# A transformer decoder layer on one core: first loads on ScalarE's queue, one batch's tokens fetched earlier, one weight load cut in four

## The chip, the core and the metric

The kernel runs on one NeuronCore of one Trainium2 chip. A core has TensorE (PE: matrix products into PSUM), VectorE (DVE), ScalarE (ACT), GpSimd (POOL) and SyncE (SP), which run side by side and wait for each other by semaphores. Loads and stores between HBM and SBUF are issued by SP or ACT into a queue each and carried out by the core's 16 DMA engines. The metric is the device time of one launch in microseconds (us): the median of runs without a profiler. Times inside an execution come from one profiled execution, counted from its span's start.

## The reference

One decoder layer in f32: x (16 batches of 512 tokens of 256), then three parts, each with a residual and a layer norm.

```
# self-attention without softmax, 16 heads of 16, K = 2
q  = x + x @ Wq + bq
ks = x + x @ Wk[k] + bk[k];  vs = x + x @ Wv[k] + bv[k]      (both / 32)
state = prod_k( ks[k]^T vs[k] )  per head;  out = layernorm(q @ state) * g + b;  out = out @ Wo + bo
x = layernorm(x + out)
# cross-attention, 16 heads of 64, 64 context rows per batch
q = x @ Wq.T;  k, v = split(context @ Wkv.T);  out = softmax(q k^T / 8) v;  out = out @ Wout.T + b_out
x = layernorm(x + out)
# 8 experts, each takes the first 1024 tokens with a positive routing weight
w = softmax(x @ router_w.T + router_b)
x = layernorm(x + sum_e w[:, e] * relu(x @ inter[e]) @ outw[e])
```

## The kernel before

Everything is f32. Nothing is looped on the chip in the main part: Python writes the whole layer out, batch by batch. A batch's 512 tokens are 4 tiles of 128. Weights and per-batch products are folded where they can be: the self-attention state is built from the Gram matrix of a batch's tokens (`gram`: `ps_g`, in two passes at L634 and L639, and a transpose `ps_gt`, L650), times Wk (`ps_gk`), times Wv (`ps_s`), masked to heads (`state`, L744 and L745), and folded with Wq into one matrix (`ps_m`, L757), which multiplies the transposed tokens (`ps_o`, L775). Keys of the cross-attention (`ps_kv`, L511, from the transposed context `cT` and transposed rows of Wkv, `wT`) are made for all batches in the first 110 us and stored to DRAM (`k_dram`); so are the values times Wout (`vo_dram`). The cross-attention reads them back per batch (`ps_sim`, `ps_x`). Experts (`ps_h` L1077, `ps_e` L1094) run on the first two batches' tokens, held in SBUF as `x2_head` and, transposed, `head_T`.

What sets the order of instructions: six generators ("streams": grams, context, self-attention, cross-attention, routing, experts) yield between pieces of work. `weave` always advances the stream whose due time (`plan`) is earliest, among those that a small cost model (`Model`) holds to be ready; `until(lambda: made(t))` makes a stream yield until the model thinks that tile t is there. The model has its own notion of when a load lands: a load issued by ACT is there 5 us later, one issued by SP early on adds up in a line. `in_order` then fixes the resulting order on PE, DVE, ACT and POOL. DMA issues on SP are not part of that; SP takes its own in the order that the tile framework gives, one after another, each waiting for what it needs, among them the DMA semaphore that it takes over from an earlier DMA (eight of them are handed round).

The steps that matter here, with lines of this version:

- L218 loads ACT's function table as ACT's first instruction.
- L359 loads batch b's tokens for its Gram matrix (`gx`); batch 0 in four pieces, at the very start. Batch 1's load is the sixth of SP.
- L1239 issues the first two context tiles (`cn`, L490) and the first two tiles of Wkv's rows (`nat`, L500), 512 KB each, alternately, all on SP behind batch 0's `gx`.
- `key_weights` (L386) and, as the streams run, `rest_of_weights` (L424) load the other weights.
- After batch 1's Gram matrix, `finish_key_weights` and `router_columns` prepare Wk and the router's columns.
- `self_attention` loads a batch's tokens again, `xt` (L694), right ahead of their use; batch 0 needs them for a transpose on PE (L249) and for the residual.
- `routing(0)` (L966) closes the pool `setup`, opens the pool `ffn` in its room and loads the first expert's inner weights `wi` (L1111, 1 MB) and outer weights `wo_` (L1116, 1 MB). The first of these two waits until all that used the old room is done.
- `experts` waits, in the model, for both weights, and then writes out eight blocks of 128 inner features, 2 matmuls each, per 256 tokens.

Of the kernel before, what the change touches and what calls it, by code (L numbers as in the profile page):

```python
# [18 lines left out]
P = 128  # L19
# [105 lines left out]
def decoder_layer(  # L125
# [25 lines left out]
    nc = tc.nc  # L151
# [12 lines left out]
    E, _, FF = w_inter.shape  # L164
    NF = FF // P
# [48 lines left out]
        return t  # L214

    nc.scalar.preload_act_table_set("natural_log_exp_and_others")  # L218
    ident = const.tile([P, P], FP, tag="ident", name="ident")
    make_identity(nc, ident)  # L220
    eps = const.tile([P, 1], FP, tag="eps", name="eps")
# [107 lines left out]
    with ExitStack() as att:  # L329
# [66 lines left out]
        def finish_key_weights():  # L396
            for k in range(K):
                plus_identity(wk[:, :, k, :])

            nc.vector.tensor_scalar_mul(nbk, nbk, float(S))  # L400
# [5 lines left out]
            out=hm, in_=hm, pattern=[[0, NC], [-HD, P // HD], [0, HD]], compare_op=ALU.is_ge,  # L406
# [3 lines left out]
            out=hm, in_=hm, pattern=[[0, NC], [HD, P // HD], [0, HD]], compare_op=ALU.is_ge,  # L410
# [74 lines left out]

        BJ = B * J

        def load_context(sp, q):
            t = wk2.tile([P, 4, C], FP, tag="vo", name="cn", bufs=6)
            nc.sync.dma_start(  # L490
                out=t,
                in_=context.rearrange("b j c -> (b j) c")[q * 512:(q + 1) * 512, :].rearrange(
                    "(i p) c -> p i c", p=P
                ),
            )
            return t

        def load_wkv(sp, r4):
            t = wk2.tile([P, 4, C], FP, tag="vo", name="nat", bufs=6)
            nc.sync.dma_start(out=t, in_=x_wkv[r4 * 512:(r4 + 1) * 512, :].rearrange("(r p) c -> p r c", p=P))  # L500
            return t

        NG = 512 // (GB * J)
# [183 lines left out]
                    sums[b // QB][1].append(key_sums(sums["u4"]))  # L687
                    yield WAIT

        grams, sums, x_blocks = {}, {}, {}  # L690

        def load_x(b):
            t = wk1.tile([P, NT, CX], FP, tag="xt", name="xt")
            nc.sync.dma_start(out=t[:, :, :C], in_=x[b].rearrange("(t p) c -> p t c", p=P))  # L694
            return t

        def self_attention(b, done):
# [47 lines left out]
            nc.vector.scalar_tensor_tensor(state, state, STATE_SCALE, headmask, ALU.mult, ALU.mult)  # L745

            yield from until(lambda: finished["x1"] >= b)
            xt = load_x(b)
            if b < FIRST:
                yield from until(lambda: made(xt))  # L750
                transposed(xT.rearrange("p t c n -> p c t n"), xt, lambda t: t)
# [212 lines left out]
        head_T, first_expert, ffn = {}, [], None  # L964

        def routing(b, x1):  # L966

            nonlocal ffn
            x2 = x2_head[:, b] if b < HEAD_B else x1
            yield from normalized(x2, lambda t: x1[:, t, :])  # L970
            yield WAIT
            if b == 0:

                yield from until(lambda: ("values", 1) in held)
                setup.close()
                ffn = pool(att, "ffn", 1)
                first_expert.extend((load_inter(0), load_outer(0)))
            if b < HEAD_B:
                head_T[b] = ffn.tile([P, NC, S], FP, tag=f"head_T{b}", name="head_T", bufs=1)
                transposed(head_T[b], x2)  # L980
            yield
            w = w_all[:, b * NT:(b + 1) * NT, :]
            m = small.tile([P, NT], FP, tag="rm", name="rm")
            mbc = m.unsqueeze(2).to_broadcast([P, NT, E])
            nc.vector.tensor_add(w, x2[:, :, C:], cs["rb"].unsqueeze(1).to_broadcast([P, NT, E]))
            nc.vector.tensor_reduce(m, w, AX.X, ALU.max)
            nc.vector.tensor_sub(w, w, mbc)
            nc.scalar.activation(w, w, AF.Exp)
            yield WAIT
            nc.vector.tensor_reduce(m, w, AX.X, ALU.add)  # L990
            nc.vector.reciprocal(m, m)
            nc.vector.tensor_mul(w, w, mbc)
            if b >= HEAD_B:


                r0 = (b - HEAD_B) * S
                nc.sync.dma_start(out=x2_rest[r0:r0 + S, :].rearrange("(t p) c -> p t c", p=P), in_=x2[:, :, :C])
                yield from normalized(x2[:, :, :C], lambda t: x2[:, t, :C])
                nc.sync.dma_start(out=out[b].rearrange("(t p) c -> p t c", p=P), in_=x2[:, :, :C])
            yield  # L1000
# [59 lines left out]
        def experts():  # L1060

            wi = wo_ = None
            yield from until(lambda: 0 in head_T and made(head_T[0]))
            for e in range(E):
                if e == 0:
                    wi, wo_ = first_expert
                    yield from until(lambda: made(wi, wo_))
                for n in range(CAP // TB):  # L1070
                    b, t0 = divmod(n * TB // P, NT)
                    yield from until(lambda: b in head_T and made(head_T[b]))
                    hT = []
                    for f in range(NF):
                        ps = bank("ps_h")
                        for cc in range(NC):
                            nc.tensor.matmul(  # L1077
                                ps[:, :TB], wi[:, cc, f * P:(f + 1) * P],
                                head_T[b][:, cc, t0 * P:t0 * P + TB], start=(cc == 0), stop=(cc == NC - 1),
                            )  # L1080
                        h = ffn.tile([P, TB], FP, tag="hT", name="hT", bufs=12)
                        if scalar_first():
                            nc.scalar.activation(h, ps[:, :TB], AF.Relu)  # L1083
                        else:
                            nc.vector.tensor_relu(h, ps[:, :TB])
                        hT.append(h)
                        yield
                    if n == CAP // TB - 1 and e + 1 < E:
                        wi = load_inter(e + 1)
                    yield from until(lambda: finished["routing"] > b)  # L1090
                    for t in range(TB // P):
                        ps = bank("ps_e")
                        for f in range(NF):
                            nc.tensor.matmul(  # L1094
                                ps[:, :C], hT[f][:, t * P:(t + 1) * P], wo_[:, f, :],
                                start=(f == 0), stop=(f == NF - 1),
                            )
                            if f % 4 == 3:
                                yield
                        acc = x2_head[:, b, t0 + t, :C]  # L1100
                        nc.vector.scalar_tensor_tensor(
                            acc, ps[:, :C], w_all[:, b * NT + t0 + t, e:e + 1], acc, ALU.mult, ALU.add
                        )
                        if e == E - 1:
                            beside(experts_st, last_norm(b, t0 + t))
                    if n == CAP // TB - 1 and e + 1 < E:
                        wo_ = load_outer(e + 1)

        def load_inter(e):
            t = ffn.tile([P, NC, FF], FP, tag="wi", name="wi", bufs=1)  # L1110
            nc.sync.dma_start(out=t, in_=w_inter[e].rearrange("(c p) f -> p c f", p=P))  # L1111
            return t

        def load_outer(e):
            t = ffn.tile([P, NF, C], FP, tag="wo_", name="wo_", bufs=1)
            nc.sync.dma_start(out=t, in_=w_out[e].rearrange("(f p) c -> p f c", p=P))  # L1116
            return t
# [60 lines left out]
        def made(*tiles):  # L1178
            return all(model.made[t.name][0] <= model.free["PE"] for t in tiles)

        def until(ready):
            while not ready():
                yield 0.5

        def all_grams():
            for b in range(B):
                if b >= QB:
                    grams_st.plan(SETUP + (b - QB - 0.8) * STEP, STEP, 2.9)
                yield from until(lambda: finished["states"] > b - 5)
                yield from grams_of([b])  # L1190
                if b == 1:
                    yield from until(lambda: made(early, wk, nbk))
                    finish_key_weights()
                    yield from router_columns(rw)
                    yield
                if b == QB - 1:
                    cs.update(rest_of_weights(sp))
                    yield
                    yield from until(lambda: made(early, wo, wv))
                    finish_weights()  # L1200
                    yield WAIT
                    yield from router_weights(sp)
# [33 lines left out]

        setup = ExitStack()
        sp = pool(setup, "setup", 2)
        nats = [load(sp, q) for q in range(2) for load in (load_context, load_wkv)]  # L1239
        gram_x[1] = load_gram_x(1)  # L1240
        key_weights()
        cs = {}
# [49 lines left out]
    with tc.For_i(0, n, 1) as i:  # L1292
# [6 lines left out]
        for e in range(E):  # L1299
            wi, wo_ = expert_weights(e)  # L1300
# [43 lines left out]
```

## Time and profile before

| | |
|---|---|
| three runs | 1355.06, 1355.67, 1358.25 us |
| median | 1355.67 us |
| the profiled execution | 1358.28 us, of which the span 1356.3 us |
| mean granted TensorE clock over the span | 0.996 |
| HBM read, written | 127.29 MB, 49.81 MB |
| DMA, mean over the span | 132 GB/s |

The page gives busy time by engine, the chain of work that ended last, followed back from the last instruction, the costliest groups of instructions, and DMA issues with the time from issue to landing. A row of the timeline reads: start in us, how long the group lasted, engine, source line, operation, what it writes and reads, count, and in brackets the idle time of its engine ahead of it and what ended that. PEld is the load of weights into PE, SPq and ACTq are the queues' issues. A window row gives the stretch, its length, busy time of PE, PEld, DVE, ACT and POOL (with the number of instructions), the granted TensorE clock, the DMA engines' busy share and GB/s. Some lines from the start, where the loads named above stand:

```profile
0.82 1.82 SPq L359 DMA_DIRECT2D gx<-in_x_dram  x4
...
3.16 0.51 SPq L500 DMA_DIRECT2D nat<-in_L_xattn_Wkv_dram  x1
3.71 0.51 SPq L490 DMA_DIRECT2D cn<-in_ctx_dram  x1
4.26 0.51 SPq L500 DMA_DIRECT2D nat<-in_L_xattn_Wkv_dram  x1
...
59.39 1.06 PE L249 MATMUL ps_t<-ident,xt 128*128 128x128 f32 x8 [1.35 <-DMA xt<-in_x_dram]
```

### The profile page before, as it was taken

To read this page: it belongs to the slowest core of one execution; us is meant where nothing else is said; L and a number is where in the kernel's file an instruction comes from. 1 tells how busy PE (TensorE), PEld (TensorE's weight loads), DVE (VectorE), ACT (ScalarE), POOL (GpSimd) and SP (SyncE) were. 2 spreads that over 40 slices of the span, in tenths; PEclk is the share of its full clock that TensorE was granted. 3 is DMA by queue.
4 is the path that set the end of the run, shared out by engine and by line. 5 is a ranking of instruction groups with operands and counts; after the bars stand their busy time and mean duration, and the time that the engine had idled before them with its cause. 6 is when DMAs were issued, how large, how long until landed. Compare 5 with 4: busy or idle time off the path is not lost.

```text
span 1356.3 us, 23928 instructions
## 1 busy us (share of the span) xinstructions
PE 1334.3 (98%) x9438; PEld 1052.6 (78%) x9438; DVE 817.4 (60%) x1961; ACT 422.5 (31%) x970; POOL 204.2 (15%) x140
## 2 busy tenths in 40 slices
PE   8999998999999999999999999999999999999997
PEld 5676675887788787887788787877788787878796
DVE  1265837556474747567555758566655848474844
ACT  2244424242222514143222414142323304142323
POOL 0010201112021111202021111202111112112100
PEclk9999998999999999999999999999999999999999
DMA  8737474421535353723645353623635153605411
GB/s 264 210 128 241 159 225 157 118 74 41 151 119 150 110 152 96 205 70 112 172 128 142 95 154 124 185 64 110 182 88 155 63 160 109 176 30 126 129 56 41
DMA packets 115204, 178.73 MB, mean 132 GB/s; under 512 B 17032, under 2 KB 83856, under 8 KB 115088
## 3 DMA queue, kind: packets, MB, share of 16 engines
q1 hardware_dynamic: 97808, 151.98, 39.1%
q10 hardware_dynamic: 17280, 25.17, 5.5%
q8 instruction: 76, 1.25, 0.4%
q14 instruction: 40, 0.33, 0.1%
HBM read 127.29 MB, written 49.81 MB: 131 GB/s over the span
## 4 chain that ended last, share of the span: by engine, by line
PE 93%; DVE 4%; DMA 1%; issue 1%; ACT 1%; SPq 0%; POOL 0%; POOLq 0%; DVEq 0%; ACTq 0%
PE ps_x L954 17%; PE ps_h L1077 16%; PE ps_sim L933 15%; PE ps_e L1094 15%; PE ps_p L799 4%; PE ps_o L775 4%; PE ps_kv L511 4%; PE ps_gk L712 4%; PE ps_vo L571 2%; PE ps_kq L862 2%; PE ps_s L724 2%; PE ps_g L634 2%; PE ps_m L757 1%; PE ps_zt L788 1%; PE ps_g L639 1%; PE ps_t L249 1%
## 5 line engine op out<-in xcount | busy, mean ns | idle before, releaser
L1077 PE MATMUL ps_h<-head_T,wi 128*128 128x256 f32 x1024 | 243.4, 383 | 4.0 <-issue 4.0
L933 PE MATMUL ps_sim<-kq,x1T 128*128 128x512 f32 x512 | 237.8, 593 | 0.0
L1077 PEld LDWEIGHTS ps_h<-head_T,wi 128*128 128x128 f32 x1024 | 194.2, 192 | 49.8 <-issue 20.9
L954 PE MATMUL ps_x<-vo,pT 32*128 32x264 f32 x4096 | 232.5, 383 | 0.2 <-DVE off L321 0.2
L954 PEld LDWEIGHTS ps_x<-vo,pT 32*128 32x128 f32 x4096 | 209.5, 185 | 20.8 <-issue 2.3
L920 POOL TENSOR_TENSOR s<-s,sm 128x1024 f32<-128x1024 f32 x64 | 121.7, 1901 | 650.2 <-DVE sm L919 572.5
L961 DVE TENSOR_TENSOR x<-ps_x,x 128x264 f32<-128x264 f32 x64 | 23.2, 425 | 234.9 <-PE ps_x L954 234.9
L1083 ACT ACTIVATE hT<-ps_h 128x256 f32<-128x256 f32 x177 | 67.7, 382 | 302.3 <-PE ps_h L1077 266.8
L933 PEld LDWEIGHTS ps_sim<-kq,x1T 128*128 128x128 f32 x512 | 96.2, 190 | 77.7 <-issue 69.8
L939 DVE TENSOR_REDUCE mx<-ps_sim 128x8 f32<-128x512 f32 x128 | 86.2, 674 | 59.4 <-PE ps_sim L933 58.6
L911 ACT ACTIVATE s<-s 128x512 f32<-128x512 f32 x128 | 79.3, 624 | 88.9 <-DVE s L940 68.9
L940 DVE TENSOR_TENSOR s<-ps_sim,mx 128x512 f32<-128x512 f32 x128 | 88.5, 692 | 4.4
L922 DVE STREAM_TRANSPOSE pT<-s 128x1024 f32<-128x1024 f32 x64 | 78.5, 1226 | 4.5 <-POOL s L920 4.2
L918 DVE TENSOR_REDUCE sm<-s 128x16 f32<-128x1024 f32 x64 | 76.5, 1196 | 0.0
L324 ACT ACTIVATE x<-x,off,rstd 128x264 f32<-128x264 f32 (+1 forms) x112 | 58.4, 592 | 33.9 <-DVE off L321 29.5
L775 PE MATMUL ps_o<-m,xT 128*128 128x264 f32 x256 | 63.6, 389 | 0.0
L799 PE MATMUL ps_p<-wo,zT 128*128 128x264 f32 x256 | 62.0, 387 | 0.0
L799 PEld LDWEIGHTS ps_p<-wo,zT 128*128 128x128 f32 x256 | 48.5, 190 | 15.4 <-issue 6.6
L511 PE MATMUL ps_kv<-cT,wT 128*128 128x512 f32 x128 | 59.6, 596 | 0.3
L835 POOL TENSOR_TENSOR x<-x,bout 128x1056 f32<-128x1056 f32 x16 | 39.1, 2446 | 136.4 <-PE ps_t L249 43.2
L712 PE MATMUL ps_gk<-wk,g 128*128 128x256 f32 x256 | 59.4, 379 | 0.0
L712 PEld LDWEIGHTS ps_gk<-wk,g 128*128 128x128 f32 x256 | 48.5, 190 | 11.2 <-issue 4.9
(178 smaller groups left out, 1739.8 us busy)
## 6 DMA issues: line engine op xcount, KB each, us to landing
vo<-vo_dram SPq DMA_DIRECT2D x512, 132.0 KB, 4.1
vo_dram<-vst SPq DMA_DIRECT2D x64, 264.0 KB, 2.8
x_blocks<-xb ACTq DMA_DIRECT2D x24, 512.0 KB, 3.3
xt<-in_x_dram SPq DMA_DIRECT2D x16, 512.0 KB, 3.8
wi<-L_ffn_experts_inter_dram SPq DMA_DIRECT2D x8, 1024.0 KB, 4.8
x_rest<-x SPq DMA_DIRECT2D x14, 512.0 KB, 3.1
out_dram<-x SPq DMA_DIRECT2D x14, 512.0 KB, 4.5
gx<-in_x_dram SPq DMA_DIRECT2D x52, 128.0 KB, 3.8
```

Of the source, the lines that this page charges most:

```text
L511: nc.tensor.matmul(ps, wT[:, cc, r % 4 * P:(r % 4 + 1) * P], cT[:, cc, q * 512:(q + 1) * 512], start=(cc == 0), stop=(cc == NC - 1),)
L712: nc.tensor.matmul(ps[:, :C], blk, wk[:, j, k, :], start=(j == 0), stop=(j == NC - 1))
L775: nc.tensor.matmul(ps[:, :CX], xT[:, t, cc], m[:, cc, :], start=(cc == 0), stop=(cc == NC - 1))
L799: nc.tensor.matmul(ps[:, :CX], zT[:, cc, t * P:(t + 1) * P], wo[:, cc, :], start=(cc == 0), stop=(cc == NC - 1))
L911: nc.scalar.activation(s[:, hs, :], s[:, hs, :], AF.Exp, scale=SCALE)
L920: nc.gpsimd.tensor_mul(s, s, sm.unsqueeze(2).to_broadcast([P, NH, J]))
L933: nc.tensor.matmul(ps, x1T[:, t, cc], kq[:, cc, hf * 512:(hf + 1) * 512], start=(cc == 0), stop=(cc == NC - 1),)
L939: nc.vector.tensor_reduce(mx[:, hs], sim, AX.X, ALU.max)
L940: nc.vector.tensor_sub(s[:, hs, :], sim, mx[:, hs].unsqueeze(2).to_broadcast([P, 8, J]))
L954: nc.tensor.matmul(ps[q][:, :CX], probsT[pq, blk].rearrange("p t i -> p (t i)"), vos[c][pq, i, :], start=(c == 0 and i == 0), stop=(c == 7 ...
L1077: nc.tensor.matmul(ps[:, :TB], wi[:, cc, f * P:(f + 1) * P], head_T[b][:, cc, t0 * P:t0 * P + TB], start=(cc == 0), stop=(cc == NC - 1),)
L1094: nc.tensor.matmul(ps[:, :C], hT[f][:, t * P:(t + 1) * P], wo_[:, f, :], start=(f == 0), stop=(f == NF - 1),)
```

## The change

Four edits. The first context tile and the first tile of Wkv's rows are issued by ACT instead of SP, as ACT's first instructions; ACT's table load follows them. Batch 0's tokens `xt` are loaded at the point where the router's columns are prepared, behind batch 1's Gram matrix, instead of inside `self_attention`. The first expert's `wi` is loaded in four pieces of 256 of its 1024 columns (the other experts' in one). `experts` no longer waits in the model for the first expert's weights.

```
-    nc.scalar.preload_act_table_set("natural_log_exp_and_others")
...
-        def load_context(sp, q):
+        def load_context(sp, q, eng=nc.sync):
             t = wk2.tile([P, 4, C], FP, tag="vo", name="cn", bufs=6)
-            nc.sync.dma_start(
+            eng.dma_start(
...
-        def load_wkv(sp, r4):
+        def load_wkv(sp, r4, eng=nc.sync):
             t = wk2.tile([P, 4, C], FP, tag="vo", name="nat", bufs=6)
-            nc.sync.dma_start(out=t, in_=x_wkv[r4 * 512:(r4 + 1) * 512, :].rearrange("(r p) c -> p r c", p=P))
+            eng.dma_start(out=t, in_=x_wkv[r4 * 512:(r4 + 1) * 512, :].rearrange("(r p) c -> p r c", p=P))
...
-        grams, sums, x_blocks = {}, {}, {}
+        grams, sums, x_blocks, first_x = {}, {}, {}, []
...
             yield from until(lambda: finished["x1"] >= b)
-            xt = load_x(b)
+            xt = first_x.pop() if b == 0 else load_x(b)
...
-                first_expert.extend((load_inter(0), load_outer(0)))
+                first_expert.extend((load_inter(0, NF // 2), load_outer(0)))
...
                 if e == 0:
                     wi, wo_ = first_expert
-                    yield from until(lambda: made(wi, wo_))
...
-        def load_inter(e):
+        def load_inter(e, pieces=1):
             t = ffn.tile([P, NC, FF], FP, tag="wi", name="wi", bufs=1)
-            nc.sync.dma_start(out=t, in_=w_inter[e].rearrange("(c p) f -> p c f", p=P))
+            n_ = FF // pieces
+            for i in range(pieces):
+                nc.sync.dma_start(
+                    out=t[:, :, i * n_:(i + 1) * n_],
+                    in_=w_inter[e, :, i * n_:(i + 1) * n_].rearrange("(c p) f -> p c f", p=P),
+                )
             return t
...
                     yield from until(lambda: made(early, wk, nbk))
+                    first_x.append(load_x(0))
                     finish_key_weights()
...
-        nats = [load(sp, q) for q in range(2) for load in (load_context, load_wkv)]
+        nats = [load(sp, q, (nc.scalar, nc.sync)[q]) for q in range(2) for load in (load_context, load_wkv)]
+
+        nc.scalar.preload_act_table_set("natural_log_exp_and_others")
```

## The prediction

> **What bounds the kernel now.** I read the page first (busy shares, chain that ended last), then TensorE's list of waits, then the timeline and stretches of windows around each wait.
>
> ```profile
> PE 1334.3 (98%) x9438; PEld 1052.6 (78%) x9438; DVE 817.4 (60%) x1961; ACT 422.5 (31%) x970; POOL 204.2 (15%) x140
> ...
> PE 93%; DVE 4%; DMA 1%; issue 1%; ACT 1%; SPq 0%; POOL 0%; POOLq 0%; DVEq 0%; ACTq 0%
> ```
>
> TensorE (PE) is busy for 98% of the span and makes 93% of the chain: 1356.3 - 1334.3 = 22 us of idle time is all that loads can give back, except where PE is busy but slow. Where it waits:
>
> ```profile
> PE ps_h L1077 <- issue: 4.0, 1, 4.0
> PE ps_g L634 <- DMA gx<-in_x_dram: 2.9, 1, 2.9
> PE ps_m L757 <- DVE state L745: 2.4, 2, 1.2
> PE ps_t L249 <- DMA cn<-in_ctx_dram: 1.8, 1, 1.8
> ...
> PE ps_t L249 <- DMA xt<-in_x_dram: 1.4, 1, 1.4
> ```
>
> The columns are total us, times, longest. Lines 1, 4 and 5 are the three waits that the three edits touch. The one called "issue" is the first expert:
>
> ```profile
> 214.62 0.38 SPq L1111 DMA_DIRECT2D wi<-L_ffn_experts_inter_dram  x1
> ...
> 216.13 0.68 DVE L201 COPY head_T<-ps_t 128x512 f32<-128x512 f32 x1
> ...
> 219.68 6.48 PE L1077 MATMUL ps_h<-head_T,wi 128*128 128x256 f32 x16 [4.05 <-issue]
> ```
>
> The load of wi is issued at 214.62 and takes 4.8 us (its row of the DMA issues); its landing at 219.42 is what releases PE, since the other operand is there at 216.81. PE has been idle since 215.63. Next, 16 matmuls take 6.48 us, which at the 379 ns and less of this line elsewhere (8 in 1.89 at 241.62) would be 3.6. The windows (last three columns: granted clock, DMA share, GB/s) say why:
>
> ```profile
> 218.00:218.50 0.50, 0.00 (x0) 0.00 (x0) 0.50 (x3) 0.00 (x0) 0.11 (x1) 0.99 1.01 418
> 218.50:219.00 0.50, 0.00 (x0) 0.00 (x0) 0.50 (x2) 0.00 (x0) 0.50 (x1) 0.50 1.01 406
> ...
> 225.00:225.50 0.50, 0.50 (x3) 0.42 (x2) 0.00 (x0) 0.33 (x2) 0.50 (x1) 0.68 0.37 123
> ```
>
> The granted clock falls to 0.50 at 218.49, 2.86 us after the last matmul, and is back at 225.32. From 219.68 to 225.32 PE works 5.64 us at half clock: 2.8 us lost over and above the wait. It is the only such place but the kernel's tail, where the clock falls 2.31 us after the last matmul (1349.41 to 1351.72).
>
> **The change, part by part.** Compared instruction by instruction, the built programs have the same order on DVE and POOL; PE has one group moved; ACT gains two DMA issues; SP's loads are re-ordered in the first 60 us, and wi becomes four. So with PE as the bound, what is taken from a PE wait moves the end by as much, if nothing is late in its place.
>
> *Batch 0's tokens (xt).* Before: issued at 54.71, landed 59.26, PE idle 1.35 us to 59.39. Now it is issued behind the third gx load, near 15 us, over 40 us early. Gain 1.35 us; bounds 0 and 1.35. What is late next is ps_m L757, which needs state (DVE, done at 59.68): PE would reach it at 58.04 + 2 x 0.9 = 59.8, so nothing. Its issue, 0.43 us, stands on SP ahead of the k_dram stores and two gx loads; their covers are long: the third gx landed near 20.4 (14.96 + 5.4) for use at 26.3, the fourth near 27 for 33.5, and k_dram is read back at 59.34 for PE at 124.4. The other SP moves (small rows, k_dram) have the same cover.
>
> *wi in four.* Piece 0 is 256 KB. No row shows such a load on an idle queue: the nearest are 128 KB (first gx piece, issued 0.82, used 2.92: 2.1 us) and 1024 KB (4.8 us). By the line between them a piece takes 2.1 + 2.7 / 7 = 2.5; I take 2.9, since in this load's own windows the first 250 KB had moved by 217.0, 2.4 us after issue. PE starts at about 217.75 instead of 219.68: 1.9 us. Bounds: 0 (it lands no sooner) and 2.8 (head_T at 216.81). Pieces 1 to 3 follow 0.4 us apart, against 1.7 us of matmuls a piece: covered. Three more issues put wo_ off from 215.05 to about 216.2; landed at 222.2, used first at 248.6. The dropped wait in experts() changes no order.
>
> *The half clock.* PE would be back 2.1 us after its last matmul. Known: the 1.83 us wait for cn left it fast (transposes after it 276 ns, 272 elsewhere); no fall came sooner than 2.31. I take no fall: 2.8 us saved; bounds 0 and 2.8.
>
> *First loads on ACT's queue.* Taken alone it removes the 1.83 us wait for cn and, as gram 1 now stands ahead of the four ps_kv, the 0.37 us wait for wT: best case 2.2 us. But see the start:
>
> ```profile
> 2.69 0.43 SPq L490 DMA_DIRECT2D cn<-in_ctx_dram  x1
> ...
> 4.81 1.28 SPq L359 DMA_DIRECT2D gx<-in_x_dram  x1
> ...
> 8.55 1.06 PE L249 MATMUL ps_t<-ident,cn 128*128 128x128 f32 x8 [1.83 <-DMA cn<-in_ctx_dram]
> ...
> 20.33 1.05 PE L639 MATMUL ps_g<-gx 128*128 128x129 f32 x8
> ```
>
> ```profile
> 2.00:3.00 1.00, 0.05 (x1) 0.08 (x1) 0.04 (x1) 0.10 (x1) 0.68 (x3) 1.00 0.79 247
> ...
> 4.00:5.00 1.00, 1.00 (x4) 0.82 (x3) 0.00 (x0) 0.00 (x0) 0.00 (x0) 1.00 0.51 142
> ...
> 6.00:7.00 1.00, 0.71 (x2) 0.00 (x0) 0.00 (x0) 0.00 (x0) 0.00 (x0) 1.00 1.05 372
> ```
>
> From 5 us on the DMA engines are full at some 372 GB/s; from 2 to 5 they moved 213 on average. A second queue fills that hole and no more: (372 - 213) x 3 us = 0.47 MB, or 1.2 us for everything behind. cn lands sooner, gram 0's pieces (now sharing with cn) a little later. nat, used at 10.34, must still come through 1.57 MB and half of the second cn: no gain. The second gx load is now wanted sooner: before, gram 1 ran at 15.15, after four ps_kv; now ahead of them, at 11.5. That load was issued at 4.81 and took 9.4 us: landed 14.2. Now its issue waits for cn's landing (the DMA semaphore it takes over), about 7 to 8 us, but behind fewer bytes: 14.2 - 1.2 = 13.0. Then gram 1 (1.74) and eight ps_kv (2 x 3.43) bring PE to L639 at 13.1 + 8.6 = 21.7, where it was at 20.4: 1.2 us worse. With the full best case, 2.2 better; with landing still at 14.2, 2.4 worse. I take a cost of 1.0. ACT's two issues (0.35 each by its x_blocks row) put its table load (1.28) off to end near 3; ACT's first copy is at 9.21: covered.
>
> The Trainium skill, "DMA: Bandwidth & Descriptors", section "Issuing engines are not separate DMA queues", says that loads issued from several engines run on the same 16 DMA engines and only save issue time. By that rule this edit would save no more than the 0.47 MB hole, as worked out from the windows; with queues of their own it would be the 2.2.
>
> *Sum.* -1.35 - 1.9 - 2.8 + 1.0 = -5.05 us. The profiled execution took 1358.28 (span 1356.3 and 2.0 around it): 1353.2. It lies 2.6 over the median of 1355.67 (runs 1355.06, 1355.67, 1358.25). I take that as a difference of the execution elsewhere and put the sum to the median, as a wait of 4.05 is longer than any after which the clock fell: 1355.67 - 5.05 = 1350.6.
>
> **The rivals.**
> A. The half clock isn't in the median. 2.6 is close to 2.8: the two quick runs may not have paid it, or the shorter wait still takes the clock down. Then 1355.67 - 1.35 - 1.9 + 1.0 = 1353.4. For it: one run of three lies at the profiled time. Against: those executions have the same 4.05 us wait. The three changes of clock lie 6.83 and 1126.40 us apart, 2 and 330 times 3.413: it is reviewed on a fixed beat. The Trainium skill, "TensorE: Matmul & The Clock Gate", Part 1, calls that beat free-running, not reset by a kernel; by that rule where the wait falls on it differs per execution, and A's time would come up in some of them.
> B. The start costs more: slower. The second gx lands as late as before, 14.2; PE has nothing from 11.48 on, 2.7 us; from 13.8 (11.48 + 2.31) the clock falls there too. 2.4 + 2.8 - 1.35 - 1.9, with the first expert still at half clock: +2.0, 1357.6. Against: the load stands behind fewer bytes.
> C. The start gives all its 2.2: 1355.67 - 1.35 - 1.9 - 2.8 - 2.2 = 1347.4. Needs the second gx by 10.5; 3.1 MB at 372 GB/s alone last till then.
> D. The pieces don't help: the first matmul still waits for all eight DMA semaphores in the program, and if piece 0 lands with the rest only xt counts: 1355.67 - 1.35 + 1.0 = 1355.3.
>
> **Chances.** Forecast 0.50 (its own range 1349 to 1352.3), A 0.27, B 0.06, C 0.10, D 0.07. The bound of 0.3% is 4.07 us (about what a measurement of this kernel tells from no change). Faster (below 1351.6): 0.45 of the forecast, C, 0.03 of A: 0.58. Slower: most of B, 0.05. The rest is 0.37. The range, 1347.4 to 1355.0, leaves out B, part of D and the end of C.
>
> **What would show it.** xt: no PE wait near 58. wi: ps_h starts about 2.1 us after PE's last transpose, granted clock 1.00 after it, 16 matmuls in 3.6 us. Start: cn's wait gone, a DMA wait of 1 to 2 us ahead of gram 1, L639 near 21.5. I am wrong if L639 comes before 19 or after 23, or if the clock falls all the same.

## The result, and the profile after

| | before | after |
|---|---|---|
| median | 1355.87 us (1355.06 to 1359.63, 13 runs) | 1353.3 us (1352.39 to 1354.16, 13 runs) |
| ratio, 95% interval | | 0.9975 (0.9967 to 0.9983) |
| profiled execution, its span | 1358.28, 1356.3 us | 1354.12, 1352.3 us |

The change takes 2.6 us off the median, less than the 4.07 us that were set as the bound of "no change". The interval of the ratio leaves out 1, so the kernel is faster, if by little. It was forecast to take 5.05.

The page of the changed kernel, busy time and engines of the chain that ended last:

```profile
PE 1333.8 (99%) x9438; PEld 1052.6 (78%) x9438; DVE 816.6 (60%) x1961; ACT 422.7 (31%) x970; POOL 204.3 (15%) x140
...
PE 94%; DVE 4%; ACT 1%; issue 0%; DMA 0%; POOL 0%; SPq 0%; POOLq 0%; DVEq 0%; ACTq 0%
```

TensorE's idle time went from 22.0 to 1352.3 - 1333.8 = 18.5 us, and its busy time fell by 0.5 only, though the first expert's half clock is gone: slow matmuls came up elsewhere. TensorE's list of waits of the changed kernel (total us, times, longest):

```profile
PE ps_g L632 <- DMA gx<-in_x_dram: 5.1, 3, 4.0
...
PE ps_h L1074 <- issue: 1.9, 1, 1.9
```

The rows for cn and xt are no longer there. The wait for wi fell from 4.0 to 1.9. Batch 0's tokens (gx) rose from one wait of 2.9 to three of 5.1. The first expert, from the timeline, and a window of it (last three columns: granted clock, DMA share, GB/s):

```profile
60.35 1.04 PE L247 MATMUL ps_t<-ident,xt 128*128 128x128 f32 x8
...
215.77 1.92 SPq L1110 DMA_DIRECT2D wi<-L_ffn_experts_inter_dram  x4
...
218.65 3.69 PE L1074 MATMUL ps_h<-head_T,wi 128*128 128x256 f32 x16 [1.89 <-issue]
```

```profile
217.50:218.50 1.00, 0.00 (x0) 0.00 (x0) 1.00 (x2) 0.00 (x0) 0.00 (x0) 1.00 1.03 363
```

The transposes of xt have no idle time ahead of them. ps_h comes 1.89 us after the last transpose instead of 4.05, the clock stays at 1.00, and the 16 matmuls take 3.69 us instead of 6.48. Now the start: TensorE's first matmuls before, then ACT's two issues and TensorE in the changed kernel:

```profile
2.95 3.77 PE L634 MATMUL ps_g<-gx 128*128 128x257 f32 x8 [2.95 <-DMA gx<-in_x_dram]
```

```profile
0.82 0.48 ACTq L488 DMA_DIRECT2D cn<-in_ctx_dram  x1
1.32 0.53 ACTq L498 DMA_DIRECT2D nat<-in_L_xattn_Wkv_dram  x1
...
3.96 1.20 PE L632 MATMUL ps_g<-gx 128*128 128x257 f32 x2 [3.96 <-DMA gx<-in_x_dram]
5.58 1.23 PE L632 MATMUL ps_g<-gx 128*128 128x257 f32 x2 [0.42 <-DMA gx<-in_x_dram]
7.50 2.08 PE L632 MATMUL ps_g<-gx 128*128 128x257 f32 x4 [0.70 <-DMA gx<-in_x_dram]
9.38 1.92 PE L247 MATMUL ps_t<-ident,cn 128*128 128x128 f32 x8
...
14.20 1.91 PE L632 MATMUL ps_g<-gx 128*128 128x257 f32 x8
...
22.80 1.05 PE L637 MATMUL ps_g<-gx 128*128 128x129 f32 x8
```

The DMA issues of the first 16 us, before and after (KB each, median us to landing), have batch 0's four pieces as:

```profile
gx<-in_x_dram SPq DMA_DIRECT2D x4, 128.0 KB, 2.3
```

```profile
gx<-in_x_dram SPq DMA_DIRECT2D x4, 128.0 KB, 4.3
```

Before, the first 8 matmuls started at 2.95 and ran without a gap. Now 1 MB is put on the DMA engines at 0.82 and 1.32 us, beside batch 0's four pieces of 128 KB: these come late, in three groups, and the matmuls after them still run at half speed (transposes 1.92 us for 8, 1.06 at full clock). The second pass of gram 1, L639 before and L637 now, is at 22.80 instead of 20.33: 2.5 us lost at the start. Gram 1 itself, at 14.20, waits for nothing; its load (issued 5.16, 6.9 us to landing) has been there since 12.03.

Of the difference of the profiled spans, 4.0 us, the start takes back what xt gives and more: x_head's transposes stand 1.1 us later than before. From there to the end of the first expert's first block the changed kernel wins 2.16 of wait and 2.8 of half clock.

### The profile page after: what moved, and what is told of

It reads as the page before. It is cut to its first block, busy times and chain, and to the rows that moved or that the text cites. A ratio compares the mean times of both kernels' runs of the same rounds, so it can differ in the third digit from the quotient of the medians.

```text
span 1352.3 us, 23937 instructions
## 1 busy us (share of the span) xinstructions
PE 1333.8 (99%) x9438; PEld 1052.6 (78%) x9438; DVE 816.6 (60%) x1961; ACT 422.7 (31%) x970; POOL 204.3 (15%) x140
## 3 DMA queue, kind: packets, MB, share of 16 engines
q8 instruction: 76, 1.25, 0.4%
## 4 chain that ended last, share of the span: by engine, by line
PE 94%; DVE 4%; ACT 1%; issue 0%; DMA 0%; POOL 0%; SPq 0%; POOLq 0%; DVEq 0%; ACTq 0%
PE ps_x L952 17%; PE ps_h L1074 16%; PE ps_sim L931 16%; PE ps_e L1091 15%; PE ps_p L797 4%; PE ps_kv L509 4%; PE ps_o L773 4%; PE ps_gk L710 4%; PE ps_vo L569 2%; PE ps_kq L860 2%; PE ps_s L722 2%; PE ps_g L632 2%; PE ps_m L755 1%; PE ps_g L637 1%; PE ps_zt L786 1%; PE ps_t L247 1%
## 5 line engine op out<-in xcount | busy, mean ns | idle before, releaser
L1074 PE MATMUL ps_h<-head_T,wi 128*128 128x256 f32 x1024 | 240.6, 380 | 1.9 <-issue 1.9
```

What stands on the lines that cost most here:

```text
L1074: nc.tensor.matmul(ps[:, :TB], wi[:, cc, f * P:(f + 1) * P], head_T[b][:, cc, t0 * P:t0 * P + TB], start=(cc == 0), stop=(cc == NC - 1),)
```

## The experiments

"Eight", "four" are the pieces of the first expert's wi; "start" is the edit with ACT's queue and the table load. Ratios are against runs of the kernel before on the same chip: runs 1 to 4 share one, 5 to 8 another, 9 to 11 a third, and 12 has a fourth.

**1. The kernel before, once more** (no edit).

> The kernel before, unchanged, to see how its executions differ. Theory: the half clock at the first expert (2.8 us) is paid in some executions and not, or less, in others, because the clock is reviewed on a fixed beat that a launch doesn't reset; then the runs spread over 1355.0 to 1359.6 us, the long ones (over 1357) have the lower mean granted clock (0.996) and the short ones a higher one (0.998 or more). Rival: the clock falls there in every execution and the spread is something else; then all runs show a mean clock near 0.996, whatever their time. Ratio 1.000 in both.

Measured: 1355.66 us (1355.05 to 1359.66, 11 runs), ratio 1.0003 (0.9994 to 1.0012), profiled 1356.94. Its start and its first expert:

```profile
6.69 1.94 PE L249 MATMUL ps_t<-ident,cn 128*128 128x128 f32 x8
...
19.45 1.05 PE L639 MATMUL ps_g<-gx 128*128 128x129 f32 x8
...
218.76 6.16 PE L1077 MATMUL ps_h<-head_T,wi 128*128 128x256 f32 x16 [4.14 <-issue]
```

There is no wait for cn at all, and L639 stands at 19.45, not 20.33. cn landed 3.9 us after issue here (3.8 to 4.1 in runs 3, 4, 7, 8 and 11), 5.7 in the execution that the prediction read. The 1.83 us that the start edit aimed at belong to that one execution. The half clock at ps_h is there again: from 218.76 to 223.77. The three runs over 1357 us have a mean granted clock of 0.995 to 0.997, the eight others one of 0.997 or 0.998. That is the theory's direction, but the groups overlap, and the mean also counts the fall in the kernel's tail, where TensorE has no matmul left (4.6 us of before's profile, 1.5 of this one). So it does not tell where the long runs lose.

**2 and 3. Start alone; four pieces alone.** Each is its part of the diff shown above, nothing else.

> Only the first context tile and the first tile of Wkv's rows go over ACT's queue (its table load behind them). Theory: this part alone costs the 2.4 us by which L639's second pass came later (22.8 instead of 20.3): batch 0's gx pieces share the DMA engines with them and come in up to 3 us later, and PE, interrupted, stays at half clock to about 13 us. Then that pass stands near 22.8 here too, the wait for xt near 58 us stays, and the median is 2 to 2.5 over the kernel before (ratio 1.0015 to 1.0018). Rival: the cost comes from the xt load and the other moves on SP; then this part gains its 1.8 us and the pass stands near 18.5 (ratio 0.9987).

> Only the first expert's inner weights come in four loads. Theory: PE's wait there falls from 4.05 to 1.9 us, the clock falls there seldom or never, everything ahead of it is as before. Median 2.1 us under the kernel before plus what the half clock cost in the median run (0 to 2.8): 1351.0 to 1353.8, ratio 0.996 to 0.9985, and a smaller spread of the runs (under 2 us instead of 4.5). Rival (the clock falls in every execution of before): 4.9 us, ratio 0.9964, the low end.

| | median (range, runs) | ratio | profiled |
|---|---|---|---|
| 2, start | 1357.87 (1357.21 to 1361.63, 11) | 1.0018 (1.0009 to 1.0027) | 1361.63 |
| 3, four | 1353.36 (1351.15 to 1354.05, 11) | 0.9978 (0.9969 to 0.9987) | 1353.36 |

The start alone makes the kernel slower, by 2.2 us against the runs of before on this chip (1355.67), as the theory had it. Its profile has the late token pieces (waits of 0.47 and 0.82), L639 at 22.75, and no wait for xt, since TensorE now comes late enough for it: part of the loss hides there. The clock also falls once near 75 us in that execution, which is part of its 1361.63.

Four pieces alone bring 2.3 us instead of the 4.7 that the two steps of the prediction sum to. The profile of run 3 shows one reason, first expert and windows of it:

```profile
216.20 5.38 PE L1076 MATMUL ps_h<-head_T,wi 128*128 128x256 f32 x16 [1.88 <-issue]
```

```profile
216.00:216.50 0.50, 0.30 (x1) 0.34 (x2) 0.50 (x1) 0.00 (x0) 0.00 (x0) 0.87 0.84 277
216.50:217.00 0.50, 0.50 (x2) 0.35 (x2) 0.47 (x3) 0.00 (x0) 0.00 (x0) 0.50 0.85 188
...
219.50:220.00 0.50, 0.50 (x3) 0.39 (x2) 0.50 (x3) 0.49 (x2) 0.00 (x0) 0.72 1.09 389
```

The wait is 1.88 us, as in the changed kernel. Yet the clock falls, at 216.37, when TensorE is already back at work, and returns at 219.78: 1.7 us lost. With a wait of 1.9 us it stayed up in the profiles of the changed kernel and of runs 4, 5, 6 and 10. So 1.9 us of idle time may or may not take the clock down. The runs spread over 2.9 us, where under 2 were expected.

**4. Early tokens and four pieces, without the start** (all loads on SP).

> The changed kernel with the first loads back on SP, as before; xt early and wi in four kept. Theory: the start is as before (second pass L639 near 20.4), no wait near 58 us, ps_h starts 1.9 us after the wait begins: 2.0 to 2.4 under the changed kernel, 1351.0 (ratio 0.9964 to the kernel before). Rival (the start's cost hangs on the early xt load): the pass stands near 22.8 and the time at 1353.3, ratio 0.998.

Measured: 1351.92 us (1350.85 to 1352.88, 8 runs), ratio 0.997 (0.996 to 0.9981), profiled 1350.85: L639 at 19.30, ps_h after 1.91 us of wait, 3.69 us for the 16 matmuls, no fall. That is 0.9 over the 1351.0 expected. It beats the changed kernel by leaving out one of its edits. Against run 3, on the same chip, the early tokens are worth 1353.36 - 1351.92 = 1.44 us.

**5 and 6. The changed kernel again; the table load ahead of ACT's loads** (L1244 moved back to the top).

> The changed kernel unchanged, on one chip with the next three. Median 1353.3 again. In its first profile the second pass L639 stood at 22.8, against 19.3 without the loads on ACT, though the medians differ by 1.4 only (1353.3 against 1351.9). Theory: PE, held up by late gx pieces, comes out of half clock later or sooner by where the fixed beat falls, so this pass moves between executions, 21 to 23, and the price of the start with it (1.4 to 3.4). Rival: it is a fixed 3.4 from the DMA traffic and the pass stands at 22.7 to 22.9 again.

> The changed kernel with ACT's table load again ahead of its two loads, so that the first context tile is issued at about 2.1 instead of 0.82 us. Theory (sharing: the loads on ACT take the DMA engines from gx): the gx pieces issued up to 2.6 us then come in as in the kernel before, the first matmul starts near 3.0 instead of 3.7 to 4.0, L639's second pass near 20 to 21, median 0.7 to 1.4 under the changed kernel, 1352.0 to 1352.6, ratio 0.997. Rival (what costs is a second queue in itself, or gram 1 ahead of the keys): as the changed kernel, 1353.3, ratio 0.998.

Run 5: 1353.3 us (1352.36 to 1354.23, 10 runs), ratio 0.9977 (0.9968 to 0.9986); profiled 1353.9, L639 at 22.52. That pass has moved by 0.3 us only, too little to tell the theory from the rival. Against run 4 the start costs 1.4 us in the medians, or 1.25 when each is set against before on its own chip. Run 6: 1353.25 us (1352.55 to 1353.9, 10 runs), ratio 0.9976 (0.9967 to 0.9985). It missed its aim: ACT's queue issued cn at 0.85 all the same, while the table load ran from 0.82 to 2.10, so neither load was put off. SP's order changed instead, with batch 1's tokens issued at 2.69, ahead of the second context tile. The run tells nothing of the two theories.

**7 and 8. Early tokens with eight pieces; early tokens alone** (both with all loads on SP).

```
-                first_expert.extend((load_inter(0, NF // 2), load_outer(0)))
+                first_expert.extend((load_inter(0, NF), load_outer(0)))
```

> xt early and the first expert's inner weights in eight loads of 128 KB, first loads on SP as before. Theory: the clock falls when PE is idle for over half of one beat of 3.41 us (1.68 us in one beat left it, 1.88 us took it down); the first piece lands 0.3 to 0.5 us sooner, the wait is 1.4 to 1.6 us, under half a beat, and the clock never falls there: median 1350.3 to 1350.8 and little spread there, 1.2 to 1.6 under the kernel with four loads (1351.9), ratio 0.9962. Rival (a fall hangs on the idle time itself, not on a share of a beat, or eight issues delay the pieces): 1351.5 to 1352, ratio 0.997, and executions with a fall remain.

> Only batch 0's tokens are loaded early. Theory: the wait of 1.2 to 1.35 us near 58 us goes and nothing comes in its place; the first expert is as before. Median 1354.3 (ratio 0.999), spread as in the kernel before (over 4 us). Rival: the other moves on SP, or a load that comes in another's way, give part back: 1355 or more.

| | median (range, runs) | ratio | profiled |
|---|---|---|---|
| 7, early, eight | 1350.4 (1349.47 to 1351.48, 6) | 0.9956 (0.9943 to 0.9969) | 1349.47 |
| 8, early | 1355.45 (1353.88 to 1357.24, 12) | 0.9994 (0.9986 to 1.0003) | 1355.38 |

Run 7 is the best so far, and its median is the one that the theory gave. Its first expert:

```profile
214.60 3.69 PE L1076 MATMUL ps_h<-head_T,wi 128*128 128x256 f32 x16 [1.43 <-issue]
```

The wait is only 0.48 us shorter than in run 4, the median 1.5 lower. The rest would be executions in which four pieces still paid for the clock, as run 3's did, but this is not shown. Three of run 7's own six executions took 1351.0 to 1351.5, with a mean clock of 0.997 to 0.998 against 0.999 in the others, and none of these three was profiled. Run 8 is inconclusive: 0.35 us in the medians and 1.1 between the lowest runs (before: 1355.0), with a ratio of 1 inside the interval. Its median lies where the rival had it, at 1355 or more. Its profile has the xt wait gone (transposes at 56.60 with no idle time) and the half clock as before, from 217.03 to 222.72, 6.50 us for the 16 matmuls.

**9 and 10. What in the start costs.** Both keep the changed kernel's order on TensorE. Run 9 has the tokens' four pieces first, two on each queue, then the first cn on SP and nat on ACT, and eight pieces; run 10 sends the second pair over ACT instead of the first, with four pieces as in the changed kernel.

```
-                    eng.dma_start(
+                    (nc.scalar if b == 0 and i % 2 else eng).dma_start(
...
-        nats = [load(sp, q, (nc.scalar, nc.sync)[q]) for q in range(2) for load in (load_context, load_wkv)]
+        nats = [load_context(sp, 0), load_wkv(sp, 0, nc.scalar), load_context(sp, 1), load_wkv(sp, 1)]
```

```
-        nats = [load(sp, q, (nc.scalar, nc.sync)[q]) for q in range(2) for load in (load_context, load_wkv)]
+        nats = [load(sp, q, (nc.sync, nc.scalar)[q]) for q in range(2) for load in (load_context, load_wkv)]
```

> The changed kernel's order on TensorE (gram 1 ahead of the first four ps_kv), tokens early, wi in eight, but the first loads dealt otherwise: batch 0's four token pieces first, two on each queue, then the first context tile on SP and the first tile of Wkv's rows on ACT. My theory (the start of the changed kernel is late because the 512 KB loads stand beside the token pieces, not because a second queue is used): token pieces landed by about 2.9 us, first Gram matmul near 3.0, no waits of 0.4 us or more between them, L639's second pass at 19.0 to 19.4, and a median as the run with wi in eight and all loads on SP, 1350.0 to 1350.6 (ratio 0.996). Rival (a second queue in itself, or gram 1 ahead of the keys, costs): L639 near 22 and 1.4 us more, 1351.8 (ratio 0.997).

> The changed kernel, but the second context tile and the second tile of Wkv's rows go over ACT's queue as its first instructions, and the first pair stays on SP behind the token pieces. My theory (sharing): the token pieces come late as in the changed kernel (first Gram matmul 3.3 us or later, waits of 0.4 us or more between the pieces), though nothing early needs what ACT loads; the first pair is late behind it; L639's second pass at 22 or later; median 1353 to 1354 (ratio 0.9975 to 0.9985). Rival (the late start comes from the first pair itself leaving SP, not from sharing): token pieces as in the kernel before, L639 near 19.3, median 1351.9 (ratio 0.997).

Run 9: 1354.16 us (1352.18 to 1356.8, 11 runs), ratio 0.9988 (0.9979 to 0.9997). My theory fell, and the rival came, with L639 at 21.75. The median is even 2.4 over the rival's 1351.8; the profiled execution also loses 1.7 us to a fall of the clock at 327.56. The token pieces are fairly quick (first matmul 3.45, no gap after it), but the start is late all the same; its timeline:

```profile
8.39 1.06 PE L247 MATMUL ps_t<-ident,cn 128*128 128x128 f32 x8 [1.36 <-DMA cn<-in_ctx_dram]
...
13.07 1.98 PE L632 MATMUL ps_g<-gx 128*128 128x257 f32 x8 [1.74 <-DMA gx<-in_x_dram]
...
21.75 1.05 PE L637 MATMUL ps_g<-gx 128*128 128x129 f32 x8
```

cn comes late, and gram 1, now ahead of the keys, waits 1.74 us for its load, which took 9.4 us from issue. This is the wait that the prediction had expected in the changed kernel.

Run 10: 1354.0 us (1352.04 to 1356.26, 11 runs), ratio 0.9986 (0.9977 to 0.9995). As my theory had it: first matmul 3.31, a wait of 0.74 between the pieces, one of 0.79 for cn, gram 1 without a wait at 13.44, and L639 at 22.05, though nobody needs early what ACT loads here. So 512 KB issued at 0.85 us beside the pieces delay them: they take 3.8 us to landing, against 2.2 in run 11. ACT's second load was issued only at 3.19, when the first piece had landed.

**11 and 12. Eight pieces again; the order alone.** Run 11 is run 7. Run 12 is run 11 with one untruth told to the model that orders the work: it books the first pair as ACT's. No load moves, and TensorE has the changed kernel's order.

```
+            early = kind == "InstDMACopy" and engine != "Activation" and any(
+                n.startswith(("cn", "nat_", "nat")) and not n.startswith("nato") for n in names[1]
+            ) and self.quick > 0
+            if early:
+                self.quick -= 1
+                engine = "Activation"
             if kind == "InstDMACopy" and engine == "Activation":
```

> The run with tokens early, wi in eight and all loads on SP once more, to stand beside the two others on one chip: median 1350.4 (ratio 0.9955 to 0.9965), ps_h about 1.4 us after the last transpose with the clock at 1.00 after it. Its longer runs (1351.0 to 1351.5 in the first) carried a mean clock of 0.997 to 0.998 where the shorter had 0.999: if such a run is profiled, a fall of the clock stands at another wait than ps_h's.

> Tokens early, wi in eight and all loads on SP, as the run before it, but with the changed kernel's order on TensorE, gram 1's first pass ahead of the first four ps_kv (the model that orders the work is told that the first pair lands as from ACT's queue; no load moves). Theory (the place of gram 1 costs by itself, since its 512 KB load, issued at 4.8 us, lands about 8 us later): first Gram matmul 3.0, everything up to gram 0's transpose at 10.3 as in the run with wi in eight, then a wait of 1.5 to 3 us for gx ahead of gram 1, L639's second pass at 21 to 22, median 1352 to 1353 (ratio 0.997 to 0.998). Rival (only the sharing of the DMA engines by the second queue costs): no wait of 1 us ahead of gram 1, L639 at 19.0 to 19.6, median 1350.1 to 1350.5 (ratio 0.996).

| | median (range, runs) | ratio | profiled |
|---|---|---|---|
| 11, early, eight | 1350.1 (1349.79 to 1350.36, 5) | 0.9958 (0.9945 to 0.9972) | 1349.79 |
| 12, order only | 1353.5 (1351.81 to 1355.86, 11) | 0.9981 (0.9972 to 0.999) | 1353.5 |

Run 11 had L639 at 19.38 and ps_h after 1.39 us at full clock. None of its runs reached 1351, so the longer executions of run 7 were not met again. Run 12, timeline of the start (its line numbers are 7 higher than those of before) and a window:

```profile
9.49 0.27 PE L657 MATMUL ps_gt<-ident,g 128*128 128x128 f32 x1
12.56 3.08 PE L641 MATMUL ps_g<-gx 128*128 128x257 f32 x8 [2.80 <-DMA gx<-in_x_dram]
...
22.93 1.05 PE L646 MATMUL ps_g<-gx 128*128 128x129 f32 x8
```

```profile
14.00:15.00 1.00, 1.00 (x3) 0.73 (x3) 0.00 (x0) 0.00 (x0) 0.00 (x0) 0.50 0.99 314
```

TensorE is done with gram 0 at 9.76 and then waits 2.80 us for gx; the keys, which run 11 began at 10.67, stand behind gram 1. The clock falls in addition (16 matmuls of ps_kv follow partly at half speed). The order alone makes L639 3.55 us later than run 11, and the median 3.4 us higher, both a little more than the theory had. This is rival B's mechanism at the start, the wait and the fall of the clock, without any load on ACT's queue.

## Why the prediction was right and wrong

**What held.** The direction and the range. xt: no wait near 58, and 1.44 us between runs 4 and 3 for the 1.35 of the sum (run 8 alone can't tell). wi: 1.9 predicted, 4.05 - 1.89 = 2.16 in the profiles; ps_h 1.9 us after the transposes, 3.69 us for the 16 matmuls. Position of L639: "near 21.5", found at 22.80, 22.52 and 21.63 in three profiles of the changed start. Set against the profiled execution's own time the sum gives 1358.28 - 5.05 = 1353.2, and the changed kernel's profiled execution took 1354.12. That 1353.2 also meets the median of 1353.3 is luck, as the terms below show.

**The step that failed** is the one that moved the sum: "I take that as a difference of the execution elsewhere and put the sum to the median". Two of the terms were sizes of that one execution, and the median has them in other sizes. The time that came is rival A's, 1353.4, but that it fits to 0.1 us is luck too: A puts the half clock at nothing and the start at 1.0, where the account below has 1.55 and 2.55, two misses that cancel.

- *The start, +1.0.* It was reckoned from L639 at 20.33, where that execution's late cn had put it. Six other executions with all loads on SP and before's order (runs 1, 3, 4, 7, 8 and 11) had L639 between 19.05 and 19.45. From there the changed start costs 2.2 to 3.8 us by its three profiles; between medians it is 2.2 (run 2 against before, where the wait for xt goes as well) and 1.4 (run 5 against run 4).
- *The half clock, -2.8.* The size was right for profiled executions: 5.64 us at half clock in before's and 5.0 in run 1's, so 2.8 and 2.5 lost. But "I take no fall" was too much: of six profiles with the predicted wait of 1.9, the clock fell in one, run 3. And the median of before seems to pay less than the profile, by subtraction only: runs 7 and 11 (1350.25 on average) have no xt wait, no fall at ps_h and 1.4 us of wait. Put 1.35 for xt and 4.05 - 1.4 = 2.65 for the wait on top, and 1354.25 results; before has 1355.8, which leaves 1.55 for the half clock. Run 8 speaks against it: its profiled execution lies at its median, has the same wait of 4.0 us, and is at half clock for 5.7 us, 2.8 lost.

In the same way the changed kernel should have 1350.25 + 0.5 of longer wait = 1350.75, and has 1353.3: 2.55 for the start and what falls of the clock remain. So the account reads -1.35 - 2.15 - 1.55 + 2.55 = -2.5 where the prediction had -1.35 - 1.9 - 2.8 + 1.0. This is worked out from medians; the two terms of 1.55 and 2.55 were not measured singly.

**The mechanism of the start.** The forecast had a wait of 1 to 2 us for the second gx load ahead of gram 1. In the changed kernel it isn't there; runs 9 and 12 show that it was put off, not wrong: with the token pieces quick, gram 1 waits 1.74 and 2.80 us. In the changed kernel the pieces are so late that TensorE arrives after that load. That load was issued right behind cn's landing, as forecast, but at 5.16 instead of 7 to 8, and it landed at 12.03 instead of 13.0. What the prediction had in half a sentence ("gram 0's pieces (now sharing with cn) a little later") was the larger part: gram 1 can start 3.9 us later than in run 4 (gram 0's transpose at 14.09 against 10.19). Of this 0.9 is the first piece, 1.1 the waits between pieces, and the rest slow matmuls: the clock is full from 13.63 on, in run 4 from 8.49. The Trainium skill, "DMA: Bandwidth & Descriptors", section "Issuing engines are not separate DMA queues", has loads from several engines interleave on the same DMA engines. Run 10 agrees, with 3.8 us to landing for the pieces and 0.74 us of wait between them.

**The rivals.** A came, for both of its reasons in part: the shorter wait takes the clock down in some executions (run 3), and quick executions of before seem to pay less than the profiled one (by subtraction only). B's mechanism was shown by run 12, but in the changed kernel it lies behind the later pieces. C fell: cn wasn't late in most executions, so there was nothing to give, and the second gx landed at 12.03 where C needed 10.5. Its best case of 2.2 was also a little high: the 0.37 us wait for wT is that of PEld, the weight load, and PE itself was idle for 0.14 us there. D fell: the wait shrank by 2.16 us, where D had it unchanged.

**Left open.** Whether ACT's queue would pay with before's order on TensorE wasn't tried, so what the sharing costs without the changed order isn't known. Nor was the cost of the half clock in a short execution of before seen in a profile.

The version with early tokens, eight pieces and all loads on SP beats both kernels: 1350.1 and 1350.4 us, ratio 0.9956 to 0.9958 against before, where the changed kernel has 0.9975.

## What to carry to other kernels

Before a sum from one profile is set against a median, profile the same kernel again, and see which waits are in both: here the wait that an edit was made for was in one execution of several. When a load moves to another queue, look at what it shares the DMA engines with, and at which work an ordering model pulls forward because it believes the load is there: here the order alone made the start 3.55 us later, and a large load beside small urgent ones, with that order, 2.7 (run 10 against run 11). A wait that is cut can be worth more than its length, if the clock stays up after it: from 1.9 to 1.4 us brought 1.5 between medians, though where the other 1.0 comes from wasn't shown.

## What the runs showed of the hardware

*The clock's beat.* In each of the 14 profiles the changes of the granted clock lie whole multiples of about 3.41 us apart (run 3: 216.37 and 219.78), on a grid that lies elsewhere in each. The Trainium skill, "TensorE: Matmul & The Clock Gate", Part 1, gives a free-running window of 3413 ns, which the grid bears out. The clock came up only after beats in which TensorE was idle for 0.17 us or less; a beat 72% busy did not bring it back (run 2, 221.84 to 225.25). What takes it down is less plain. Many falls came after beats with more than half idle: 1.88 of 3.41 us took the clock down (run 3), 1.68 did not (before's wait for cn, 6.87 to 10.28). But run 4 had a beat with 1.89 us idle (213.29 to 216.71) and kept its clock, and in run 2 it fell at 75.06 after a beat with 0.18 us idle. So the idle share of a beat, as the profile shows it, does not decide by itself. What can be counted is the wait at the first expert: 4.0 us took the clock down in four profiles of four (before, runs 1, 2 and 8), 1.9 us in one of six (the changed kernel, runs 3, 4, 5, 6 and 10), 1.4 us in none of four (runs 7, 9, 11 and 12).

*A fall without a long wait.* In run 9 the clock fell once in the middle of the kernel. A window of it:

```profile
328.00:329.00 1.00, 1.00 (x14) 0.80 (x13) 0.21 (x1) 0.00 (x0) 1.00 (x1) 0.50 0.63 206
```

Ahead of it TensorE waits four times for ACT's x, 0.96 and three times 0.17 us, or 1.47 us of a beat of 3.41; between the waits stand single transposes, which the busy row counts with 0.33 us each, against 0.13 in a row of eight. All versions have these waits; in the 13 other profiles the clock stayed up there, and none of them had more than 1.31 us of idle time in one beat there. Such places may be why executions of one kernel lie up to 4 us apart, which wasn't tested.

*ACT's queue isn't held by its table load.* In run 6 it issued cn at 0.85 us and nat at 1.35, while the load of the table ran from 0.82 to 2.10.
